# A hybrid attention, MLP and Mamba kernel on one core: smaller first scan parts, and the product with C issued one unit later

## The chip, the core and the metric

The kernel runs on one core of one Trainium2 chip. The core has TensorE (PE, matmuls; PEld are its weight loads), VectorE (DVE), ScalarE (ACT), GpSimd (POOL) and SyncE (SP, here a queue that issues DMAs). Each engine works through its own queue in order and waits on semaphores for the others. The metric is the device time of one execution in microseconds (us), smaller is better. A profile of one execution gives every instruction's start and end.

## The reference, cut to what matters

The input x is 4 batches of 1024 tokens of 128 channels, all float32. Four residual layers follow one another:

```python
x = x + attention(layernorm(x))   # 16 heads, window of 32 tokens and every 64th token before
x = x + mlp(layernorm(x))         # [x, -x] @ +-1 (256x512), relu * 2, @ +-1 (512x512), relu * 2, @ +-1 (512x128)
x = x + mamba(layernorm(x))
x = x + mlp(layernorm(x))

def mamba(x):                     # E = 256 inner channels, N = 16 states, kernel of 4 taps
    xn = layernorm(x) * ln_g + ln_b
    u, z = split(xn @ W_in)
    u2 = silu(causal_conv(u) + conv_b)
    dt_lo, Bm, Cm = split(u2 @ W_xp)              # 8, 16 and 16 columns
    dt = softplus(dt_lo @ W_dt + b_dt)
    for t in tokens:                              # h: (batch, E, N), zero at token 0
        h = exp(dt[t] * A) * h + (dt[t] * u2[t]) * Bm[t]
        y[t] = (h * Cm[t]).sum(over N)
    return res_scale * ((y + u2 * D_param) * silu(z)) @ W_out
```

## The kernel before, in words

**Stages.** Attention runs first, in tiles of 64 rows of two batches at once. Then come the MLP, the Mamba layer and the second MLP, interleaved. Nearly all instructions go through a helper at line 57 (InOrder), so the profile gives line 57 for them, and tiles tell them apart.

**Chunks.** x lies in SBUF as two pairs of batches (bp = 0, 1). A pair is cut into four chunks c of 256 tokens of both batches, 512 columns. The first MLP (early), the second MLP of the first pair (late) and the norm ahead of Mamba (mamba_norm) work on chunks. The MLP's tiles are fxn (normalised), ftp (its transpose in PSUM), fxnT (split in a high and a low part), pf/h1, pg/h2 (the two hidden layers) and pfo; the suffix a, b or c tells early, late and late_batch (the second MLP on single batches). Two lanes run the MLPs of alternating chunks; each is a Python generator of Pieces.

**Parts and units.** The recurrence is scanned in eight parts (parts_in_order, line 911): a part is one batch b and one half f of its tokens, 512 tokens, in the order (0,0), (1,0), (0,1), (1,1), (2,0) ... The first two parts so need chunks 0 and 1. A part has 16 units, one for each state n; 128 units in all. The last column of each state is kept in carry for the batch's second half.

**Before a part.** mamba_pre_half prepares it: gate (pz, SiLU), the convolution as four shifted matmuls (pc) and SiLU to u2, px = u2 @ W_xp, a split of B and C into bf16 parts (bc), B and C written to DRAM (bd), dt (pd, softplus) and du = dt * u2. In the very first part the gate comes last.

**A unit** (scans, from line 1246) does the following, h being the two halves of the 256 channels:
- SP loads B of two states from bd to all partitions (bs, load_b, three units ahead); POOL makes db = du * bs (drive, two units ahead).
- ACT makes da = exp(dt * A) into PSUM (decay), two buffers in all; da of the next unit's h waits until the scan of this unit's h has read it.
- DVE scans each h: hs = da * hs + db.
- PE spreads C over all partitions (pcc, one PSUM buffer), and DVE multiplies hc = hs * pcc. For states 3, 8 and 13 (BY_GP) POOL multiplies instead, with C loaded by SP (cs).
- A DMA on POOL's queue adds each second hc to its neighbour (gather), and PE sums hc into pys with an identity matmul (total). After the last state DVE multiplies the gate with pys (gate_by); then comes the output projection (mamba_out, or mamba_out_own for the second pair).

**The order** within an engine's queue is the program's order while keep is set, which holds for the scans. It comes from a small planner: each unit calls pieces() twice, which issues waiting Pieces of the other work (mamba_pre_half, mamba_norm, mamba_out, statistics, the lanes, in that order), as far as planned times, a rate for each engine (RATES: PE 2.9 us a unit, DVE 1.2, ACT 2.4, POOL 1.2) and three spare PSUM banks allow. Evictions marked lump wait for a call that takes lumps. When a part isn't prepared in time, ready() issues Pieces without regard to rates until it is.

Ahead of the scans all eight PSUM banks are free, and a plain loop runs the norm of chunks 0 and 1, the first preparation and the lanes in turn:

```python
while (*parts_in_order[0], NH - 1) not in prepared:
    ...
    wanted = first[-1].may() and "pe" in first[-1].next.us
    for w in first + ([] if wanted else lanes):
        if w.may():
            w.run()
```

Of the kernel before, what the change touches and what calls it, by code (L numbers as in the profile page):

```python
# [26 lines left out]
P = 128  # L27
# [16 lines left out]
def hybrid_kernel(ctx: ExitStack, tc: tile.TileContext, x, Wq, Wk, Wv, Wo, ln_g, ln_b, W_in, conv_w,  # L44
# [789 lines left out]

    def early(bp, c, *args):
        stats = yield from awaited(("a", bp, c))
        tiles = xs[bp][:, 4 * c : 4 * c + 4, :]
        yield from mlp(f"a{bp}_{c}", tiles, True, *args, hasty=bp == 1 and c < HALF, stats=stats)
        fed.add(("a", bp, c))
# [64 lines left out]
    carry = [mw.tile([P, NH, N], F32, name=f"carry{b2}") for b2 in range(2)]  # L904
# [6 lines left out]
    parts_in_order = [(b, f) for bp in range(NP) for f in range(2) for b in (2 * bp, 2 * bp + 1)]  # L911
# [6 lines left out]
    def mamba_norm(bp, c):  # L918
# [5 lines left out]
        before = order_of[2 * bp, f] - 4  # L924
# [4 lines left out]
        yield Piece(gp=2.7)  # L929

        rs = small.tile([P, 5, 4], F32, tag="rs2", name=f"rs_z{u}", bufs=2)
        gp.tensor_scalar_add(rs[:, 0], mv[:, :, 1], EPS)
        gp.tensor_scalar(rs[:, 1], mv[:, :, 1], 1.0 + EPS, EPS * EPS, ALU.mult, ALU.add)
        both = rs[:, 0:2].rearrange("p a n -> p (a n)")
        gp.tensor_tensor(both, both, minus_half, ALU.pow)
        gp.tensor_scalar_mul(rs[:, 4], mv[:, :, 0], -1.0)
        gp.tensor_mul(rs[:, 2:4], rs[:, 0:2], rs[:, 4:5].to_broadcast([P, 2, 4]))
        gp.tensor_scalar_add(rs[:, 0], rs[:, 0], 1.0)
# [15 lines left out]
        yield Piece(sc=1.6, same=True)  # L954
        ln_apply(tiles, tiles, rs[:, 0], rs[:, 2])
        yield evict(sc=0.6)
# [4 lines left out]
        )  # L961
        fed.add(("n", bp, c))

    def gate_of(v, gate, xnT):
        yield fill(1.8, 2, loose=True)
        pz = [bank(f"pz{v}_{h}") for h in range(NH)]
        for h in range(NH):
            te.matmul(pz[h], w_in[:, E + h * P : E + (h + 1) * P], xnT[:, DC - 1 :], start=True, stop=True)
# [4 lines left out]
    def mamba_pre_half(b, f):  # L973

        bp, b2, place = b // 2, b % 2, order_of[b, f]
        yield Piece(
            ready=lambda: all(("n", bp, c) in fed for c in range(f * HALF, (f + 1) * HALF))
# [4 lines left out]
        xnT = mamba_in[bp, f][:, b2, :]  # L982
        gate = m2.tile([P, NH, CH], F32, name=f"gate{v}", tag="gate", bufs=4)
        if place:
            yield from gate_of(v, gate, xnT)
# [12 lines left out]
        for h in range(NH):  # L998
            for k in range(DC):
# [3 lines left out]
                elif k % 2 == 0:  # L1003
                    yield Piece(pe=1.8, urgent=hurry)
                te.matmul(
                    pc[h], w_conv[:, k, h * P : (h + 1) * P], xnT[:, k : k + CH], start=k == 0, stop=k == DC - 1
                )
        yield evict(lump=True, sc=3.9)
# [18 lines left out]
        if not place:  # L1027
            yield Piece(1, evict=True, ve=1.4)
            ve.tensor_copy(bc, px[: 6 * N])
            ve.tensor_sub(res[: 4 * N], px[: 4 * N], bc[: 4 * N])  # L1030
            yield Piece(-1, urgent=hurry, sc=1.8)
        else:
            yield Piece(1, evict=True, sc=1.8)
            sc.copy(bc, px[: 6 * N])
        sc.copy(dtl[6 * N :], px[6 * N : 6 * N + DR])
        sc.copy(w, px[: 2 * N])
        nc.sync.dma_start(bd, w)
        prepared.add((b, f, "b"))
        if not place:
            sc.copy(bc[: 4 * N], res[: 4 * N])  # L1040
        else:
# [11 lines left out]
        yield evict(lump=True, sc=3.9)  # L1053
        for h in range(NH):
            sc.activation(dt[:, h], pd[h], AF.Softplus, bias=bdt_t[:, h : h + 1])
        if not place:
            ve.tensor_sub(res[: 2 * N], res[: 2 * N], bc[: 2 * N])
        yield urgent(sc=0 if place else 0.6)
        if not place:
            sc.copy(bc[: 2 * N], res[: 2 * N])  # L1060
        for h in range(NH):
            yield urgent(gp=1.3)
            gp.tensor_mul(du[:, h], dt[:, h], u2[:, h])
            prepared.add((b, f, h))
        if not place:
            yield from gate_of(v, gate, xnT)

    def mamba_out(bp, f):

        pair = [(2 * bp + b2, f) for b2 in range(2)]  # L1070
        yield Piece(ready=lambda: all(("g", *k) in fed for k in pair), same=True)
        for q in range(HALF):
            yield fill(2.0)
            po = bank(f"pmo{bp}_{f}{q}")
            for b2 in range(2):
                if b2:
                    yield more(2.0)
                gate = mamba_pre[pair[b2]][0]
                for i in range(4):
                    t0 = (4 * q + i) * R  # L1080
# [399 lines left out]
```

## Time and profile before

| | us |
|---|---|
| median of 3 runs | 893.15 |
| lowest, highest | 889.9, 897.59 |
| the profiled execution | 896.53 |
| its span, first to last instruction | 894.7 |
| last attention instructions, about | 246 |
| first scan starts | 322.9 |
| last scan ends | 852.0 |

Over the whole span PE is busy 757.9 us (85%), DVE 726.9 (81%), POOL 682.5 (76%) and ACT 606.3 (68%). These shares are means over stages with different limits, so the stages are read apart. In a line of groups the columns are engine, operation, tiles out<-in, shapes, count, busy time, mean duration in ns, and the idle time before them with what ended it. In a line of the timeline the first two numbers are the start and the length in us, and the bracket is the idle time of the engine before it. A matmul's end is modelled in the profile, so PE's busy time is not its peak rate. A float32 matmul is two instructions.

### The profile page before, as it was taken

What the parts mean: (1) busy time and instruction counts of PE and PEld (TensorE: products, weight loads), DVE (VectorE), ACT (ScalarE), POOL (GpSimd) and SP (SyncE); (2) the same over time, 40 slices, a digit from 0 to 9 for tenths busy, and PEclk for the clock granted to TensorE, in tenths of its full rate; (3) what the DMA queues carried; (4) which work ended last, traced back from release to release, by engine and by line L of the source; (5) the groups of instructions that cost most, each with busy time, mean ns of one, the idle gap of its engine ahead of it and who ended that gap; (6) DMA issues with size and microseconds to landing.
All of it is one profiled execution on the core that took longest, in us unless ns stands there. A gap on an engine that the chain in (4) does not pass through costs nothing. (4 is left out here: it accounts for less than half of the span.)

```text
span 894.7 us, 16435 instructions
## 1 busy us (share of the span) xinstructions
PE 757.9 (85%) x6204; PEld 465.8 (52%) x6204; DVE 726.9 (81%) x970; ACT 606.3 (68%) x1358; POOL 682.5 (76%) x525
## 2 busy tenths in 40 slices
PE   5798878966788977788989788989889689889898
PEld 2455546645667653334546554535545345656567
DVE  6699998999563258898899998898988779999942
ACT  3776656754364488887878778878967766664523
POOL 6689966999342079999989998979979879877800
PEclk9899989997679989797999999899989799999999
DMA  4743133330010036564564656555565545666410
GB/s 127 129 74 73 27 57 68 74 70 2 3 48 1 1 109 155 127 159 129 137 148 130 153 130 153 145 121 138 155 154 133 141 112 150 164 145 153 108 25 19
DMA packets 59808, 92.77 MB, mean 104 GB/s; under 512 B 6200, under 2 KB 39776, under 8 KB 59728
## 3 DMA queue, kind: packets, MB, share of 16 engines
q1 hardware_dynamic: 49488, 58.15, 22.6%
q0 software_dynamic: 9680, 33.30, 19.8%
q8 instruction: 49, 0.80, 0.4%
q10 hardware_dynamic: 560, 0.26, 0.1%
q14 instruction: 31, 0.25, 0.1%
HBM read 52.11 MB, written 4.72 MB: 64 GB/s over the span
## 5 line engine op out<-in xcount | busy, mean ns | idle before, releaser
L57 POOL TENSOR_TENSOR db<-du,bs 128x1024 f32<-128x1024 f32 x128 | 315.6, 2504 | 23.8 <-DVE hs L57 20.1
L57 ACT ACTIVATE da<-dt,a_t 128x512 f32<-128x512 f32 x256 | 175.2, 687 | 107.1 <-DVE hs L57 106.8
L57 DVE TENSOR_TENSOR_SCAN hs<-da,db 128x512 f32<-128x512 f32 x128 | 149.9, 1209 | 29.7 <-ACT da L57 29.5
L57 DVE TENSOR_TENSOR_SCAN hs<-da,carry,db 128x512 f32<-128x512 f32 x128 | 156.7, 1266 | 5.5 <-ACT da L57 5.2
L57 PE MATMUL pys<-hc,ident 128*128 128x512 f32 x258 | 145.3, 649 | 1.9 <-DMA hc<-hc 1.8
L57 DVE TENSOR_TENSOR hc<-hs,pcc 128x1024 f32<-128x1024 f32 x104 | 126.7, 1218 | 22.1 <-PE pcc L57 15.9
L57 POOL TENSOR_TENSOR prodv<-vS,E 128x128 f32<-128x128 f32 (+14 forms) x30 | 69.6, 2319 | 12.2 <-ACT E L57 11.9
L57 PE MATMUL pga<-h1a,w 128*128 128x512 f32 x256 | 72.4, 435 | 5.1 <-ACT u L57 2.9
L57 PEld LDWEIGHTS pys<-hc,ident 128*128 128x128 f32 x258 | 49.6, 208 | 43.6 <-issue 37.2
L57 POOL TENSOR_TENSOR prod<-kv,qs 128x128 f32<-128x128 f32 (+14 forms) x30 | 71.3, 2376 | 1.0 <-DVE or L57 1.0
L57 POOL TENSOR_TENSOR hc<-hs,cs 128x1024 f32<-128x1024 f32 x24 | 58.1, 2421 | 13.6 <-DVE hs L57 11.6
L57 PE MATMUL pc<-mxnT,w_conv 128*128 128x512 f32 x128 | 63.3, 624 | 4.3 <-DVE h1b L57 2.4
L57 PEld LDWEIGHTS pga<-h1a,w 128*128 128x128 f32 x256 | 51.2, 201 | 27.4 <-issue 4.3
L57 POOL DMA_DIRECT2D hc<-hc x63 | 62.7, 995 | 1.8 <-issue 0.9
L57 ACT ACT_TABLE_LOAD x48 | 61.6, 1283 | 3.5 <-issue 2.6
L57 PE MATMUL pcc<-bc,spread 96*128 96x512 bf16 x104 | 42.0, 404 | 22.5 <-DVE hc L57 21.7
L57 ACT ACTIVATE E<-S 128x512 f32<-128x512 f32 (+15 forms) x62 | 26.5, 472 | 38.8 <-DVE S L57 38.6
L57 PE MATMUL ps<-kx,qT 64*32 64x256 f32 x1008 | 46.2, 432 | 6.3 <-DVE S L57 5.0
L57 POOL TENSOR_TENSOR du<-dt,u 128x512 f32<-128x512 f32 x16 | 24.8, 1551 | 29.7 <-ACT dt L57 29.6
L57 PEld LDWEIGHTS pc<-mxnT,w_conv 128*128 128x128 f32 x128 | 25.2, 199 | 37.4 <-issue 31.9
L57 ACT COPY ep<-pt 128x512 f32<-128x512 f32 x32 | 18.8, 587 | 36.4 <-DVE eo L57 36.1
L57 PE MATMUL pgb<-h1b,w 128*128 128x512 f32 x128 | 38.0, 447 | 1.4 <-ACT u L57 1.4
(245 smaller groups left out, 1682.9 us busy)
## 6 DMA issues: line engine op xcount, KB each, us to landing
bs<-bd SPq DMA_DIRECT2D x64, 512.0 KB
hc<-hc POOLq DMA_DIRECT2D x63, 512.0 KB, 4.6
vr<-vd SPq DMA_DIRECT2D x32, 256.0 KB
cs<-bd SPq DMA_DIRECT2D x24, 256.0 KB
vd<-kv SPq DMA_DIRECT2D x8, 256.0 KB
x<-in_L_attn_a_x_dram SPq DMA_DIRECT2D x15, 128.0 KB
kx<-kT SPq DMA_DIRECT2D x104, 16.0 KB
out_dram<-x SPq DMA_DIRECT2D x8, 128.0 KB
```

The source lines that it names most:

```text
L57: ins = getattr(self.engine, name)(*args, **kwargs)
```

## The change

The first two parts are now called quarters: part (QUARTER, f) holds tokens f*256 to f*256+255 of batches 0 and 1 side by side, 512 columns as before. Quarter 0 needs chunk 0 alone, quarter 1 chunk 1. Chunk 0's MLP is cut in two: each lane takes two of its four tiles (256 columns). The lanes then take chunks (0,1), (0,3), (1,1), (1,3) and (0,2), (1,0), (1,2). A scan of a quarter is two instructions of 256 columns, one for each batch. mamba_norm marks a chunk as transposed ("t") ahead of its residual copy, and Mamba's preparation waits for that mark. For the first chunk some small norm operations go from POOL to DVE. In the first part the order within the preparation is another: dt's projection comes before the copy of B and C to DRAM, the small casts of bc go to POOL, du goes to DVE, and db of unit 0 is made half by DVE and half by POOL. The loop before the scans is replaced by one that runs both lanes until chunk 0 is through, and then puts norm and preparation first.

In the scans, DVE's product of unit i-1 now stands between unit i's two scans; before, the product of unit i stood behind both. The two calls of pieces() move with it: the one that takes lumps comes behind the product, the other at the unit's end; pcc is issued between them. The planner's durations of scans and products are a little smaller.

```diff
+    def early_half(lane, *args):
+        stats = yield from awaited(("a", 0, 0))
+        at = slice(2 * lane, 2 * lane + 2)
+        yield from mlp(f"a0_0{lane}", xs[0][:, at, :], True, *args, stats=stats[:, :, at])
+        fed.add(("half", lane))
+        if all(("half", k) in fed for k in range(2)):
+            fed.add(("a", 0, 0))
...
-        yield from mlp(f"a{bp}_{c}", tiles, True, *args, hasty=bp == 1 and c < HALF, stats=stats)
+        yield from mlp(f"a{bp}_{c}", tiles, True, *args, hasty=c == 1 or (bp == 1 and c < HALF), stats=stats)
...
-    parts_in_order = [(b, f) for bp in range(NP) for f in range(2) for b in (2 * bp, 2 * bp + 1)]
+    QUARTER = "quarter"
+    QT = CH // 2
+    parts_in_order = [(QUARTER, 0), (QUARTER, 1)]
+    parts_in_order += [(b, f) for bp in range(NP) for f in range(2) for b in (2 * bp, 2 * bp + 1)][2:]
...
-        yield Piece(gp=2.7)
+        by = ve if bp + c == 0 else gp
+        yield Piece(gp=2.9 if by is ve else 2.7)
...
+        needs = [("t", 0, f)] if b == QUARTER else [("t", b // 2, c) for c in range(f * HALF, (f + 1) * HALF)]
...
         for h in range(NH):
             te.matmul(pd[h], w_dt[6 * N :, h * P : (h + 1) * P], dtl[6 * N :], start=True, stop=True)
-        yield evict(lump=True, sc=3.9)
+        if not place:
+            yield Piece()
+            sc.copy(w, px[: 2 * N])
+            nc.sync.dma_start(bd, w)
+            prepared.add((b, f, "b"))
+            ve.tensor_copy(bc, px[: 6 * N])
+            ve.tensor_sub(res[: 4 * N], px[: 4 * N], bc[: 4 * N])
+            gp.tensor_copy(bc[: 4 * N], res[: 4 * N])
+            ve.tensor_sub(res[: 2 * N], res[: 2 * N], bc[: 2 * N])
+            gp.tensor_copy(bc[: 2 * N], res[: 2 * N])
+        yield evict(lump=True, sc=3.9 if place else 1.9)
...
         for h in range(NH):
-            yield urgent(gp=1.3)
-            gp.tensor_mul(du[:, h], dt[:, h], u2[:, h])
+            yield urgent(gp=1.3) if place else urgent(ve=0.6)
+            (gp if place else ve).tensor_mul(du[:, h], dt[:, h], u2[:, h])
...
+        def product(i):
+
+            if i < 0 or by_gp(i):
+                return
+            hss[i] = m2.tile([P, NH, CH], F32, name=f"hc{i}", tag="hc", bufs=6)
+            ve.tensor_tensor(
+                hss[i], hs_of.pop(i), pcs.pop(i).unsqueeze(1).to_broadcast([P, NH, CH]), ALU.mult
+            )
+            done["hc", i] = done["pcc read",] = spend("ve", 1.15, *after(("pcc", i)))
+
...
+            def scan(h):
+                da = das.pop((i, h))
+                spans = [(b2, slice(b2 * QT, (b2 + 1) * QT)) for b2 in range(2)] if b == QUARTER else [(b, slice(0, CH))]
+                for b2, ts in spans:
+                    first = carry[:, h, b2 % 2, n : n + 1] if f else 0.0
+                    ve.tensor_tensor_scan(hs[:, h, ts], da[:, ts], db[:, h, ts], first, ALU.mult, ALU.add)
+                us = (1.21 if f else 1.15) + 0.07 * (len(spans) - 1)
+                done["hs", i, h] = spend("ve", us, *after(("da", i, h), ("db", i)))
+                decay(i + 1, h)
+
+            scan(0)
+            done["da", i + 1, 0] = spend("sc", 0.67, *after(("hs", i, 0)))
+            product(i - 1)
             if gather(i):
                 spend("gp", 0.9, *after(("hc", i - 1)))
+            t = times["ve"]
+            pieces(t + 1.5)
             if not by_gp(i):
-                pc = wide.tile([P, CH], F32, name=f"pcc{i}", tag="pcc")
-                te.matmul(pc, spread[: 6 * N, n, :], mamba_pre[b, f][4], start=True, stop=True)
+                pcs[i] = wide.tile([P, CH], F32, name=f"pcc{i}", tag="pcc")
+                te.matmul(pcs[i], spread[: 6 * N, n, :], mamba_pre[b, f][4], start=True, stop=True)
                 done["pcc", i] = spend("pe", 0.4, *after(("pcc read",)))
-            hs = m2.tile([P, NH, CH], F32, name=f"hs{i}", tag="hs")
-            db = dbs.pop(i)
-            for h in range(NH):
-                first = carry[b % 2][:, h, n : n + 1] if f else 0.0
-                ve.tensor_tensor_scan(hs[:, h], das.pop((i, h)), db[:, h], first, ALU.mult, ALU.add)
-                done["hs", i, h] = spend("ve", 1.235 if f else 1.175, *after(("da", i, h), ("db", i)))
-            decay(i + 1, 0)
-            done["da", i + 1, 0] = spend("sc", 0.67, *after(("hs", i, 0)))
-
-            t = times["ve"]
-            pieces(t + 2.5, lumps=False)
...
+            scan(1)
...
-                ve.tensor_tensor(hss[i], hs, pc.unsqueeze(1).to_broadcast([P, NH, CH]), ALU.mult)
-                done["hc", i] = done["pcc read",] = spend("ve", 1.205, *after(("pcc", i)))
...
             done["sum", i] = spend("pe", total(i))
             t = times["ve"]
-            pieces(t + 2.2)
+            pieces(t + 2.0, lumps=False)
+        product(last)
...
-            early(0, lane, f1, lane, *[in_scan_buffers] * lane),
-            early(0, 2 + lane, f1, lane),
-            early(1, lane, f1, lane),
-            early(1, 2 + lane, f1, lane),
+            early_half(lane, f1, lane, *[in_scan_buffers] * lane),
+            *(early(bp, c, f1, lane) for bp, c in (((0, 1), (0, 3), (1, 1), (1, 3)), ((0, 2), (1, 0), (1, 2)))[lane]),
...
-        while (*parts_in_order[0], NH - 1) not in prepared:
+        while ("a", 0, 0) not in fed:
...
+        while (*parts_in_order[0], NH - 1) not in prepared:
+            w = lead if ("t", 0, 0) not in fed else pre
+            if not w.count:
+                w.since = lead.since
+            issue(w)
+            if pre.held and lead.next:
+                issue(lead)
+            if aside and (QUARTER, 0, "b") in prepared:
+                aside = False
+                for v in lanes:
+                    while v.next.evict or v.held:
+                        issue(v)
+            for v in lanes:
+                while aside and v.may() and max(ends(v)[0].values(), default=0.0) < w.since + 0.3:
+                    issue(v)
```

## The prediction

> **What bounds the kernel now.** I read the page first, for the span and the slices (each digit is a fortieth, 22.4 us).
>
> ```profile
> span 894.7 us, 16435 instructions
> DVE  6699998999563258898899998898988779999942
> POOL 6689966999342079999989998979979879877800
> ```
>
> VectorE (DVE) is full except in slices 11 to 15: the stretch from the end of attention (246 us) to the first scan. The table by stages shows what fills that stretch and what fills the scans.
>
> ```profile
> 323.00:388.00 65.00, 51.06 (x128) 23.46 (x128) 55.42 (x62) 57.34 (x120) 60.80 (x49) 0.82 0.48 127
> 388.00:457.00 69.00, 58.24 (x173) 29.64 (x172) 60.46 (x60) 56.19 (x127) 62.19 (x44) 0.90 0.59 149
> 457.00:588.00 131.00, 116.44 (x444) 68.61 (x443) 120.66 (x113) 107.48 (x231) 120.47 (x96) 0.94 0.56 141
> 588.00:723.00 135.00, 117.98 (x418) 63.61 (x418) 112.94 (x108) 105.06 (x242) 118.12 (x89) 0.92 0.56 141
> 723.00:852.00 129.00, 114.73 (x480) 71.65 (x479) 124.61 (x126) 79.31 (x144) 104.71 (x64) 0.95 0.57 139
> 262.00:323.00 61.00, 57.65 (x273) 42.98 (x272) 12.97 (x33) 31.19 (x57) 10.80 (x16) 0.97 0.07 23
> ```
>
> Columns after the length: PE, PEld, DVE, ACT, POOL busy with instruction counts, PE's granted clock, DMA share, GB/s. Before the scans PE is the bound (57.65 of 61) and DVE waits. From 322.9 to 852.0, 529 us for 128 units of 4.13 us, DVE is busy 474 (90%), POOL 466, PE 458, ACT 405. The scans are a DVE stage with 55 us of holes; the groups say which.
>
> ```profile
> L57 DVE TENSOR_TENSOR_SCAN hs<-da,db 128x512 f32<-128x512 f32 x128 | 149.9, 1209 | 29.7 <-ACT da L57 29.5
> L57 DVE TENSOR_TENSOR hc<-hs,pcc 128x1024 f32<-128x1024 f32 x104 | 126.7, 1218 | 22.1 <-PE pcc L57 15.9
> ```
>
> So the holes are a late decay from ACT or a late spread C from PE, never POOL. After 852 comes a fixed tail of 42.7 us (last gate, output projection, last MLP).
>
> **Step 1, the head.** Now the first part needs batch 0's tokens 0 to 511, that is chunks 0 and 1: two whole MLPs and two norms. After the change it needs chunk 0 alone, each lane taking half. What two halved lanes cost stands in the tail, where the last chunk is run just so (256 columns):
>
> ```profile
> 258.63 15.09 PE L57 MATMUL pga<-h1a,w 128*128 128x512 f32 x64
> 273.56 7.30 PE L57 MATMUL pfoa<-w,h2a 128*128 128x128 f32 x64
> ...
> 877.87 2.13 PE L57 MATMUL pfc<-fxnTc,w 128*128 128x256 f32 x16 [0.33 <-ACT fxnTc L57]
> 879.84 7.73 PE L57 MATMUL pgc<-h1c,w 128*128 128x256 f32 x64
> 887.41 3.73 PE L57 MATMUL pfoc<-w,h2c 128*128 128x128 f32 x32
> 891.18 0.48 DVE L57 SCALAR_TENSOR_TENSOR ox<-pfoc,total,ox 128x256 f32<-128x256 f32 x1 [1.30 <-PE pfoc L57]
> ```
>
> The first two lines are the pair of whole chunks, the rest the halved pair: 891.66 - 877.87 = 13.8 us from first projection to residual. Now the first MLP gets its split input at 254.3 (DVE is making spread and w_conv until 253.6; that stays), and its residuals end at 281.65. New: 254.3 + 13.8 = 268.1.
>
> Norm of chunk 0: 8 statistics 1.75, small ops with the power on POOL 2.9, apply 1.65, last transpose 0.2, scaled copy 0.77, waits 0.3: 7.6, so 275.7. (Putting the 4-element ops on DVE saves at most the 1.2 of POOL's four; I take nothing.) Now the convolution starts only at 300.98.
>
> Convolution to first scan, now 21.95 us (300.98 to 322.93): conv 7.0, SiLU 0.7, px 1.9, then dt rows and w copied (0.6 each), bd to DRAM until SP issues bs (313.38 to 315.02, 1.64), bs landing, half of db 1.2. Landing of bs isn't shown: at most 5.2 (issued 315.02, db at 320.21 waited for du, not for it), at least 2.1 (the small loads on POOL's queue); I take 4.6, what the equally large hc gathers need. Sum 18.2: first scan at 294. The other branch (pd 2.0, softplus 1.3, du on DVE 1.3, db 0.7 after px) is shorter, and the two bc casts that go to POOL (no row of such a cast; between the 0.36 of POOL's small copy into mxnT and the 1.55 of du) end before bs is there. Without that cover they cost up to 3 us. bd and bs keep their order on SP; bd now stands behind the pd matmuls, 0.6 later than dt's rows. **First scan 29 us earlier**, bounds 20 (PE's fill between norm and convolution, 4 us now, grows; bs 5.2) to 34.
>
> **Step 2, the product one unit late.** In the timeline of DVE:
>
> ```profile
> 544.25 1.22 DVE L57 TENSOR_TENSOR hc<-hs,pcc 128x1024 f32<-128x1024 f32 x1
> 545.38 2.45 DVE L57 TENSOR_TENSOR_SCAN hs<-da,carry,db 128x512 f32<-128x512 f32 x2
> 547.93 1.22 DVE L57 TENSOR_TENSOR hc<-hs,pcc 128x1024 f32<-128x1024 f32 x1
> 549.07 2.45 DVE L57 TENSOR_TENSOR_SCAN hs<-da,carry,db 128x512 f32<-128x512 f32 x2
> ```
>
> The scan begins 0.08 us before the product in front of it has ended (544.25 + 1.22 = 545.47), the two scans overlap as much, but the product begins 0.09-0.10 after the scan that it reads. That read of a result just written costs 0.09 + 0.08 = 0.173. In the whole trace 73 of 104 products follow a scan directly; the others already have another instruction between. The late product reads scans of a unit ago: 73 x 0.173 = **-12.6 us**, bounds 0 (something else holds the unit) and 104 x 0.173 = -18.
>
> The Trainium skill, page VectorE: DVE Perf Modes, section The DRAIN you can't avoid, speaks against this: chained copies with and without a semaphore between took the same time, so the dependence would cost nothing. By it this step is 0 and the sum below 12.6 worse; the rows differ, and I go by them.
>
> Behind the product on DVE's queue now stands the unit's second scan, so a late pcc holds that scan instead of the next unit's first; pcc still has two scans (2.5 us) between its buffer's release and its use, so the 15.9 us stay. The gather on POOL needs product i-1, now done 2.4 us into unit i; POOL reaches it after db (2.38). Its wait is 0 to 0.5, at most 31 us over 63 gathers, hidden in POOL's 63 us of idle time; if POOL had none, it would cost just that.
>
> **Step 3, shorter scans.** In the first 32 units each scan of 512 becomes two of 256: 64 more. No scan of 256 is in the trace. Others on DVE: h1c takes 0.417 at 256 columns and 0.673 at 512, fxnTc 0.40 and 0.67, so two halves cost 0.13 to 0.16 more, less the 0.08 overlap; the operand carry adds 0.05 (1.266 - 1.209) in half of them. 64 x 0.08 + 32 x 0.05 = **+6.6**, bounds 1.3 (0.02 each) and 10 (0.16).
>
> **Step 4, work pushed into the scans.** Before 322.9 DVE now does the evictions of chunks 0 and 1 and most of 2 and 3. After, at the scan start chunk 0 is done and chunks 1 and 2 are past their first projections. A chunk is 0.67 + 4 x 0.68 + 0.75 = 4.1 us of DVE, its norm 1.75: chunk 1 leaves 1.4 + 1.75, chunk 2 1.4, chunk 3 3.4: **+8**, bounds 4 and 12. On PE some 30 us move. I cost them at nothing, because lanes now have a hole: chunk 3's output is at 335.7, and the next fxna is at 384.7; PE is busy only 51 of the 65 us. Without the hole they'd cost what rival D says.
>
> **Step 5, the second part is late.** It now waits for chunk 1's MLP, norm and preparation. At the scan start chunk 1 lacks 4 x 2.05 + 2 x 2.0 = 12.2 us of planned PE, chunk 2 as much, and a unit is allowed 2.9: both end near unit 8 or 9. Norm takes two units (7.6), so preparation starts near unit 11 to 13, and load_b asks for it at 13. From there the rest is issued at once. Its chain was 22 us in the head, against three units (12 us) already queued: DVE stands **+10**, bounds 0 and 26 (preparation in the scans took 335.7 to 374.3, 38.6). Chunk 3 has until unit 29; no standstill taken there.
>
> **Sum.** -29 - 12.6 + 6.6 + 8 + 10 = -17. The profiled execution took 896.53 (span 894.7 and 1.8 around it): 879.5. The median is 893.15, 3.4 lower: **876 us**. Runs of before spread from 889.9 to 897.6, so a difference within 1% (9 us) can hardly be told from none.
>
> **The rivals.** B, clean hand-over: chunk 1 runs faster than planned, since the planner's PE figures are a little generous (2.05 for 8 pga matmuls that take 15.09/64 each, 1.89), step 5 is 0, and with pieces at two points a unit 7 of the 55 us of holes go: 893 - 34 = 859. For it: ACT and PE aren't full in 323:388. Against: clock 0.82 there.
>
> C, the start is given back: the chain of step 5 takes its 38.6 us, so +26 instead of +10: 892. For it: pieces wait for three spare PSUM banks, and two lanes and the preparation want two each. Against: once forced, nothing else is issued.
>
> D, slower, PE becomes the bound: PE is busy 109 of the 134 us of 323:457. With 30 more it needs 139; the granted clock there is already 0.82 and 0.90, and at a tenth less it needs 139 / 0.9 = 154, 20 over; lanes then reach the end a halved chunk later (13.8 more in the tail). 876 + 20 + 13.8 = 910. It decides once more than 25 us of PE move. Against: a convolution matmul shows 0.59 of busy time while they start 0.43 apart, so busy PE is less than full. That the change doesn't do what it says isn't likely: the first scan's place is set by what it waits for.
>
> **From cases to numbers.** A (forecast, 876) 0.48, B 0.18, C 0.17, D 0.17. B and nearly all of A are faster by over 1% (0.64), C and some of A within (0.19), D slower (0.17). All steps at their good ends give 893 - 47 = 846, all at their bad ends 893 + 28 = 921; they have separate causes, so A's own range takes half of each side, 861 to 898. The range takes in A's range, B's value and C's, short of D's: 857 to 899.
>
> **What would show it.** First hs near 294; median product starting 0.08 before its predecessor's end; 320 scans, those of 256 near 0.66 to 0.72; a DVE hole of some 10 us between 345 and 365 waiting for ACT da; the tail still 42 to 43 us. The prediction is wrong if the first scan is later than 303, if part two stands over 26 us, or if the last scan to the end is over 50.

## The result, and the profile after

The changed kernel takes 942.77 us (median of four runs, 939.52 to 945.51) against 891.74 of the kernel before beside it: a ratio of 1.0559, interval 1.0498 to 1.062. It is slower by 51 us; the prediction was 876, range 857 to 899. Two of the kernels below, plan_only and head_lanes, were profiled in an execution at a far lower granted clock (0.809 and 0.187) than their others, so only their times are used.

The page after, its span and two rows of the slices (a slice is now 23.5 us):

```profile
span 941.2 us, 16652 instructions
DVE  6799999998527961998188998599988799999222
POOL 6799948996406973798187899599998799885000
```

The dip ahead of the scans is shorter, as meant. Three things are new: a 1 in slice 16 and another in slice 20, inside the scans, and three 2s at the end in place of one 4 and one 2. The table by stages gives them lengths (columns as in the prediction: PE, PEld, DVE, ACT, POOL busy, PE's granted clock, DMA share, GB/s).

```profile
293.00:382.00 89.00, 62.62 (x187) 32.81 (x186) 56.38 (x91) 62.78 (x156) 66.44 (x60) 0.81 0.36 94
382.00:475.00 93.00, 78.92 (x274) 45.38 (x273) 67.27 (x108) 57.65 (x120) 62.00 (x49) 0.88 0.40 100
...
867.00:941.00 74.00, 62.63 (x417) 53.77 (x415) 18.71 (x50) 21.72 (x55) 2.98 (x6) 0.90 0.05 15
```

The first two rows are the two parts of 256 tokens. Before, the first two parts took 65.5 and 68.5 us; now 89.1 and 93.2. No engine is full in them, so something waits. The last row is the tail: 74 us in which PE works 63 and VectorE 19. From the trace, the times of three marks:

| | before | after | difference |
|---|---|---|---|
| first scan starts | 322.9 | 292.6 | -30.3 |
| first to last scan | 529.1 | 574.2 | +45.0 |
| last scan to the end | 42.6 | 74.4 | +31.8 |
| span | 894.7 | 941.2 | +46.5 |

("First to last scan" is called the stage below, "last scan to the end" the tail.) Not all of the first row is the change's: attention, which it doesn't touch, ends earlier in this trace, and the first MLP's norm starts on ACT at 242.7 instead of 246.3. From there to the first scan it is 76.6 us before and 49.9 after, 26.7 less. Traces of six kernels below whose head is the old one (late_only, late_room, late_lanes, before_lanes, late_hs3, plan_tight) have their first scan between 318.8 and 322.7.

In the middle row VectorE's busy time hardly changes (474.2 to 476.1); its idle time goes from 54.9 to 98.0. The timeline shows where it stands, VectorE from the end of unit 13 on and again from unit 30 on (start, length, engine, line, operation; in brackets the idle time ahead and what ended it):

```profile
344.21 1.26 DVE L57 TENSOR_TENSOR_SCAN hs<-da,db 128x256 f32<-128x256 f32 x2
370.65 2.43 DVE L57 TENSOR_TENSOR_SCAN hs<-da,db 128x256 f32<-128x256 f32 x4 [25.18 <-issue]
378.24 1.27 DVE L57 TENSOR_TENSOR_SCAN hs<-da,db 128x256 f32<-128x256 f32 x2 [5.16 <-ACT da L57]
...
463.59 2.67 DVE L57 TENSOR_TENSOR_SCAN hs<-da,carry,db 128x256 f32<-128x256 f32 x4 [20.52 <-issue]
471.18 1.39 DVE L57 TENSOR_TENSOR_SCAN hs<-da,carry,db 128x256 f32<-128x256 f32 x2 [4.92 <-ACT da L57]
```

VectorE stands still for 25.2 and 5.2 us in units 14 and 15, while the second part is prepared, and in the same way for 20.5 and 4.9 in units 30 and 31, ahead of the third: 55.8 us together. "issue" names no releaser, so the engine that the scan waits for has to be followed. The decay ended on ACT just before 370.65. ACT in the same stretch:

```profile
345.04 0.30 ACT L57 ACTIVATE waste<-x 128x128 f32<-128x128 f32 x1
...
353.66 0.19 ACT L57 ACTIVATION_READ_ACCUMULATOR waste<-x,st_fa 128x1 f32 x1
353.75 1.06 ACT L57 ACTIVATE h2a<-pga 128x512 f32<-128x512 f32 x2
...
369.87 0.69 ACT L57 ACTIVATE da<-dtquarter,a_t 128x512 f32<-128x512 f32 x1
```

and PE:

```profile
344.25 1.02 PE L57 MATMUL pzquarter<-mxnT,w_in 128*128 128x512 f32 x2
354.38 2.08 PE L57 MATMUL pzquarter<-mxnT,w_in 128*128 128x512 f32 x2 [9.11 <-ACT h2a L57]
```

Between 345.0 and 353.7 ACT computes statistics (stats_ahead) of chunks of the second pair, which nobody needs yet. ready() had been called in unit 13 and issued whatever was able. Behind them stands the eviction h2a; the trace names it as what released the second half of the second part's gate matmuls (pz, 354.4) after 9.1 us of idle PE. From the source, h2a empties a PSUM bank, and the preparation may only go on when one is spare. Then the preparation runs undisturbed, pz to the decay at 369.9, 15.5 us. The third part has no such block behind its norm, and is still late: chunk 3's residual lands at 427.9, its transposed norm at 446.3, and the db that the third part starts with begins 24 us after that.

The tail, on PE:

```profile
883.50 5.87 PE L57 MATMUL pgc<-h1c,w 128*128 128x512 f32 x24
889.21 4.02 PE L57 MATMUL pfoc<-w,h2c 128*128 128x128 f32 x32
...
907.74 6.03 PE L57 MATMUL pgc<-h1c,w 128*128 128x256 f32 x32
```

pgc and pfoc are late_batch, the lanes' second MLP of the last two batches. Before, the chunks of 512 columns among them had ended by 852, and only halved ones stood in the tail. How late the lanes run can be read from one tile: the residual x of the last chunk of the first MLP ends at 581.0 before and at 671.6 after. (This is the lanes' mark below, "last early x" in the tables.)

The groups of the two operations that the prediction counted on:

```profile
L57 DVE TENSOR_TENSOR hc<-hs,pcc 128x1024 f32<-128x1024 f32 x104 | 124.3, 1195 | 4.0 <-PE pcc L57 3.8
L57 DVE TENSOR_TENSOR_SCAN hs<-da,db 128x256 f32<-128x256 f32 (+1 forms) x128 | 114.9, 938 | 46.4 <-issue 25.2
```

The product's idle time fell from 22.1 to 4.0 us: locally the late product does what it should.

### The profile page after: what moved, and what is told of

Read it like the earlier page. It is cut to its first block, busy times and chain, and to the rows that moved or that the text cites. A ratio compares the mean times of both kernels' runs of the same rounds, so it can differ in the third digit from the quotient of the medians.

```text
span 941.2 us, 16652 instructions
## 1 busy us (share of the span) xinstructions
PE 761.4 (81%) x6244; PEld 466.8 (50%) x6244; DVE 730.2 (78%) x1048; ACT 606.0 (64%) x1361; POOL 682.3 (72%) x520
## 5 line engine op out<-in xcount | busy, mean ns | idle before, releaser
L57 POOL TENSOR_TENSOR db<-du,bs 128x1024 f32<-128x1024 f32 x96 | 239.2, 2526 | 16.8 <-DVE hs L57 11.4
L57 DVE TENSOR_TENSOR_SCAN hs<-da,carry,db 128x512 f32<-128x512 f32 (+1 forms) x192 | 201.8, 1088 | 39.4 <-issue 20.5
L57 ACT ACTIVATE da<-dt,a_t 128x512 f32<-128x512 f32 x192 | 131.4, 687 | 86.3 <-DVE hs L57 85.6
L57 DVE TENSOR_TENSOR_SCAN hs<-da,db 128x256 f32<-128x256 f32 (+1 forms) x128 | 114.9, 938 | 46.4 <-issue 25.2
L57 PE MATMUL pys<-hc,ident 128*128 128x512 f32 x194 | 104.1, 623 | 1.8 <-DMA hc<-hc 1.8
L57 POOL TENSOR_TENSOR db<-duquarter,bs 128x1024 f32<-128x1024 f32 (+1 forms) x32 | 78.2, 2472 | 6.9 <-DVE hs L57 4.9
L57 PE MATMUL pga<-h1a,w 128*128 128x512 f32 (+1 forms) x288 | 76.7, 418 | 5.7 <-DVE h1a L57 5.5
L57 POOL TENSOR_TENSOR prodv<-vS,E 128x128 f32<-128x128 f32 (+14 forms) x30 | 69.6, 2321 | 11.7 <-ACT E L57 11.5
L57 ACT ACTIVATE da<-dtquarter,a_t 128x512 f32<-128x512 f32 x64 | 43.8, 687 | 37.3 <-DVE hs L57 37.2
L57 PEld LDWEIGHTS pys<-hc,ident 128*128 128x128 f32 x194 | 37.3, 198 | 51.3 <-issue 39.7
L57 PE MATMUL pc<-mxnT,w_conv 128*128 128x512 f32 x96 | 44.8, 601 | 0.0
L57 ACT COPY ep<-pt 128x512 f32<-128x512 f32 x32 | 18.8, 587 | 35.5 <-DVE eo L57 35.2
```

The source lines that it names most:

```text
L57: ins = getattr(self.engine, name)(*args, **kwargs)
```

## The experiments

Three questions: which half of the change costs, what makes the tail longer, and where VectorE's saving goes. Theory at the start: the change's two halves don't affect each other, the late product gains some 10 us and the halved parts lose the rest to the standstills. All ratios are to the kernel before in runs beside it, with the 95% interval.

### One half at a time

**late_only** has the late product and no halved parts; the planner's numbers are those of the change.

```
-   te.matmul(pc ...); scan 0; scan 1; pieces(t + 2.5, lumps=False); product(i); pieces(t + 2.2)
+   scan 0; product(i - 1); pieces(t + 1.5); te.matmul(pc ...); scan 1; pieces(t + 2.0, lumps=False)
+   planned scan 1.21 / 1.15, product 1.15   (before: 1.235 / 1.175, 1.205)
```

> The unit's new order alone, on the parts and the head of the kernel before; the two calls of the planner have the changed kernel's allowances (1.5 and 2.0). Theory: the 0.173 us of each of the 73 products that follow their scan directly is DVE time on the bound, so the span falls by 9 to 13 us, to 878 to 884 beside 891.7 of before; first scan at 323, tail 43. Rival 1 (something else holds the unit): within 4 us of before. Rival 2 (the new order or its smaller allowances are what starves the lanes in the changed kernel): the last chunk of the first MLP ends far later than 580, the tail grows by 20 us or more, and the time is over 900.

Measured 925.64 us, ratio 1.037 (1.0355 to 1.0386). First to last scan 526.1 (before 529.1), VectorE's busy time in it down 13 us to 460.9 (in part because the lanes' evictions moved out of it), and the tail 77.8 in place of 42.6. So the half that should have gained loses 33 us, all in the tail, and rival 2 held.

**late_room** is late_only with the old allowances (`t + 2.5`, `t + 2.2`), **quarters_only** is the changed kernel with the unit's old order and numbers, **after_room** the changed kernel with the old allowances.

> As late_only, with the allowances of before (2.5 and 2.2) at the two calls of the planner. Theory: the lanes aren't held by the allowance, so within 5 us of late_only. Rival 2: 10 us or more faster than late_only, with an earlier end of the lanes' work.

> The quarters and the new head with the unit order of before. Theory: standstills of DVE ahead of the second and third part of 45 to 60 us together and a tail of 65 to 80 us come from the parts, so they are all here; the product's wait on its scan is back, so 950 to 956. Rival 2: standstills or tail shrink by 20 us or more and the time is under 930.

> The changed kernel with the allowances of before (2.5 and 2.2) at the two calls of the planner. Theory (lanes are late because two parts now need chunks that no earlier stage has made, and because a standstill issues nothing of theirs): within 8 us of 942.8, tail still over 65. Rival 2 (allowance): tail at most 55, time 915 to 930.

| | time, us | ratio | first scan | scans | tail | last early x |
|---|---|---|---|---|---|---|
| late_only | 925.64 | 1.0370 (1.0355-1.0386) | 320.4 | 526.1 | 77.8 | 645.1 |
| late_room | 913.75 | 1.0242 (1.0218-1.0265) | 321.2 | 537.3 | 51.9 | 620.1 |
| quarters_only | 932.19 | 1.0451 (1.0422-1.0480) | 295.1 | 573.2 | 65.2 | 658.4 |
| after_room | 951.07 | 1.0658 (1.0641-1.0676) | 293.7 | 585.4 | 70.8 | 663.8 |

Either half alone is slower, and each makes the tail longer: by 35.2 us (late_only) and 22.6 (quarters_only), against 31.8 with both, so the two do not add. The halved parts bring standstills without the late product too (12.4 and 20.5 us, the largest of quarters_only), but quarters_only is 10.6 us faster than the full change, not 7 to 13 slower as expected: there too the late product, with its plan, costs. A little more allowance helps late_only by 12 us, as rival 2 said, and the full change not at all (951.07, just outside its theory's 8 us).

### The tail: the lanes' plan

**late_lanes** is late_only with much more room for the lanes; **before_lanes** gives the same room to the kernel before, as a control; **plan_only** and **plan_tight** take the other way, the kernel before with the change's numbers.

```
late_lanes, before_lanes:  RATES pe 2.9 -> 4.0; pieces(t + 4.5) in both places
plan_only:                 planned scan 1.21 / 1.15, product 1.15
plan_tight:                plan_only, and pieces(t + 1.5), pieces(t + 2.0)
```

> late_only with more room for the lanes: PE's rate 4.0 instead of 2.9 a unit and allowances of 4.5 at both calls of the planner. Instructions are the same, the MLP's stand earlier among the scans. Theory (the product's wait was DVE time, but the shorter planned unit pushed MLP work out of the scans into the tail): the tail falls from 78 to 43 to 50 us, the scan stage is 525 to 545, the time 887 to 903 beside 925.6 of late_only. Rival (the order itself is slow: hs has two buffers and scans now wait for POOL's product): over 910, with the loss inside the scan stage.

> The kernel before with the same room for the lanes (rate 4.0, allowances 4.5). Control: if the lanes of before were not held back, within 8 us of before (884 to 900). If more room is a gain of its own, under 884; then late_lanes has to be compared with this kernel.

> The kernel before with nothing but the planner's durations of the changed one (scans 1.21 and 1.15, product 1.15); the order of scans and product is untouched. Theory (planned DVE time is the budget for MLP work in a unit): the lanes are later, the tail grows by 5 to 20 us, the time is 896 to 912. Rival (the planned durations don't matter): within 4 us of before.

> The kernel before in its own unit order, with only the numbers of the plan that the change brought: planned scan and product 1.21, 1.15 and 1.15 us (as in plan_only) and the allowances 1.5 and 2.0 us in place of 2.5 and 2.2. Theory, that the smaller allowance of the first call holds the lanes' matmuls back: the stage of the scans shortens to 520-526, the tail grows from 42.6 to 50-75, time 900-915. Rival, that the allowance only decides beside the new order of the calls: tail 40-47, time 882-893, as in plan_only.

| | time, us | ratio | scans | tail | last early x |
|---|---|---|---|---|---|
| late_lanes | 893.32 | 1.0027 (1.0006-1.0048) | 526.8 | 42.7 | 578.4 |
| before_lanes | 891.95 | 1.0015 (0.9994-1.0037) | 529.6 | 36.3 | 585.3 |
| plan_only | 885.05 | 0.9939 (0.9915-0.9962) | | | |
| plan_tight | 894.02 | 1.0021 (0.9994-1.0047) | 526.8 | 45.5 | 601.2 |

late_lanes settles the tail of late_only: three numbers of the plan, no instruction of the work, bring it from 77.8 back to 42.7, and the lanes' mark back to 578. The expectation for plan_only (896 to 912) was a miss, and plan_tight's rival held but for 1 us: in the old order the change's numbers cost nothing in time, though the lanes' mark comes 20 us later (601.2). So neither the planned durations nor both changes of numbers together make the old order slower; with the new places of the two calls the same numbers cost 33 us. Which step of the planner joins the two, and which of the three numbers undoes it, was not separated.

**after_mend** applies this to the full change: the room of late_lanes, the norm's Pieces of the first pair marked urgent, and no stats_ahead in a forced call during the first two parts.

```
+ RATES pe 4.0, pieces(t + 4.5) twice
+ yield Piece(..., urgent=not bp)              # three Pieces of mamba_norm
+ if forced and w is works[4] and now[0] < 2 * PER: continue
```

> The changed kernel with the lanes' room of late_lanes, the norms of the first pair's chunks let past the rates, and no statistics of the second pair issued while a part is waited for in the first two parts. Theory: tail 45 to 55 instead of 74; the standstills ahead of the second and third part shrink only a little, since the chain from transposed chunk to du is as long: 40 to 56 us; time 905 to 925. Rival (the standstills come from what is issued in front of the chain): under 20 us of standstill and under 900.

Measured 904.44 us, ratio 1.0162 (1.012 to 1.0205): 38 us of the 51 are back, past the good end of its theory in time, tail and standstills, and short of the rival's. The tail is 44.4, the standstills 11.7 + 4.7 + 13.4 + 4.9 = 34.7 in place of 55.8. Against late_lanes the head gains 26.6 (294.4 against 321.0), the stage of the scans loses 39.7 (566.5 against 526.8). The standstills are 34.7 of that. The three edits went in together, so what each is worth was not measured.

**mend_gate** moves pz and its two SiLU evictions of the second and third part behind the part's preparation (`if place: gate_of` becomes `if place > 2`, the call at the end takes the rest).

> after_mend, with the gate's two matmuls (2.1 us of PE) and their two Silu evictions (on ACT) of the second and third part moved behind the part's preparation, as the first part has it. Theory, that the standstills are in-order queues ahead of the preparation's steps: the four standstills sum to 24-31 us in place of 34.7, first to last scan 556-564, time 893-902. Rival, that the chunk's x comes too late and the chain behind it waits for other things than the gate: sum within 3 us of 34.7, time 901-908.

The standstills fell to 10.0 + 5.2 + 9.7 + 4.4 = 29.2 (from the unrounded values), as the theory said, and the time rose to 924.66, ratio 1.0363 (1.0317 to 1.0408): the tail is 57.4 and the lanes' mark 641.8 (after_mend 615.4). A miss on the time: the stage stayed at 568.5, and the lanes were later again. Why moving two matmuls and their evictions does that was not followed.

### Where VectorE's saving went

late_lanes is the late product without the long tail, and its stage is 526.8 against 529.1. Even these 2.3 us are not clear: plan_tight, in the old order, has the same 526.8. VectorE's idle time by gap, from before to late_lanes, says where the saving goes. Gaps under 0.2 us (a product behind its scan) fell from 7.3 to 1.7, busy time from 474.2 to 470.0; gaps over 0.2 us grew from 47.7 to 55.1. Its waits in the chain of waits (engine, tile, releaser: us, times, longest):

```profile
DVE hc L57 <- PE pcc L57: 20.8, 23, 2.5
...
DVE hs L57 <- ACT da L57: 16.8, 17, 2.2
...
DVE hs L57 <- POOL hc L57: 13.7, 9, 3.4
```

In before, pcc's wait was 15.9 us, and da's 34.7, of which 8.3 stand ahead of the first scan and not in the stage. The third line is new: hs has two buffers, GpSimd's product (states 3, 8 and 13) holds one, and with no product of its own behind the second scan VectorE comes sooner to the scan that overwrites it. **late_hs3** takes that wait away: `tag="hs", bufs=3`, and hc five buffers in place of six for the room.

> The late product with the lanes' allowance of late_lanes, and three buffers for hs in place of two (hc five in place of six, to make room). Theory, that the gain of the late product was lost to the scan's wait for GpSimd's product of every fifth unit, which holds one of only two hs buffers: that wait (13.7 us in late_lanes) falls under 2 us, the stage of the scans from 527 to 513-521 us, the time to 880-888. Rival, that ACT's decays and PE's spread set the pace anyway and the wait only changes its name: waits for da and pcc grow by as much, the stage stays at 524-530, the time at 889-898.

Measured 888.29, ratio 0.997 (0.9946 to 0.9995). The wait is gone, and the stage is 526.1, as the rival said; the time lies between the two bands.

```profile
DVE hc L57 <- PE pcc L57: 29.6, 32, 2.4
...
DVE hs L57 <- ACT da L57: 19.0, 20, 2.1
```

pcc and da took 11 of the 13.7 us over (29.6 - 20.8 and 19.0 - 16.8). **before_half** and **late_half** ask whether VectorE sets the stage at all.

```
- ve.tensor_tensor(hss[i], hs, pc ...)
+ ve.tensor_tensor(hss[i][:, :, : CH // 2], hs[:, :, : CH // 2], pc[:, : CH // 2] ...)
```

> The kernel before, in which VectorE's product with C computes the first 256 of 512 tokens only (PE's sum reads these twice, and the gather moves half): 104 products of about 0.67 us in place of 1.2, 55 us less on VectorE, every instruction in the same order and with the same plan. Theory A, VectorE bounds the stage: 529 falls to 474-490, time 838-855. Theory B, the stage is bound by several engines in turn (GpSimd 466 us busy, PE 459, ACT 405, in-order queues between them): the stage falls by less than half of that, to 503-520, time 865-885, and VectorE's waits for da and pcc grow.

> late_hs3 with the same halved product: 55 us less on VectorE in the order in which the product stands one unit late. Theory A: stage 526 to 471-487, time 835-852. Theory B: stage 500-518, time 862-882. If before_half gains and late_half does not, the late order has another bound than the order before.

before_half: 870.68, ratio 0.9753 (0.9703 to 0.9803), stage 507.6. late_half: 874.69, 0.9803 (0.9756 to 0.9851), stage 510.5. VectorE is busy 53 and 52 us less in the stage, and 21.5 and 15.6 us arrive (late_half against late_hs3). The page's groups of before_half:

```profile
L57 POOL TENSOR_TENSOR db<-du,bs 128x1024 f32<-128x1024 f32 x128 | 342.9, 2822 | 4.7 <-DVE hs L57 4.4
...
L57 POOL DMA_DIRECT2D hc<-hc x63 | 99.8, 1585 | 0.7 <-issue 0.4 <-POOL hc L57 0.3
```

GpSimd is busy 487.2 of the 507.6 us, 96%, with 4.7 us of idle time ahead of db (before: 23.8). Theory B's figures held in both, with one reserve: the records of the halved gather sum to 37 us more than those of the whole one (62.7 before), and db went from 2504 ns to 2822. The two lie partly over each other, and GpSimd's busy time rose by 21 us (466.4 to 487.2), so the experiment loaded GpSimd as it relieved VectorE, and the stage could not have come near theory A's 474. What it shows is that a VectorE with 53 us less to do runs into the others: in before_half its waits for da and pcc grew by 7.2 and 4.4 us, and 13.2 us of waiting for GpSimd's product, which holds an hs buffer, appear in the old order too. Where the stage would end without the load on GpSimd stays open; the test without such a load is late_hs3.

### Keeping the head's gain without halved parts

The change also shortened the first part's preparation (dt ahead of the copies of B and C, du and half of the first db on VectorE, the norm's small operations on VectorE). **head_short** is plan_only with these edits alone.

> No halved parts, no late product: plan_only with the changed kernel's edits to the first part's preparation alone (dt before the copies of B and C, du and half of the first db on VectorE, the gates of the first two chunks' norm on VectorE, the transposes evicted before the residual's norm). Theory, that the head's gain has a share that costs no standstill because the whole first half of the tokens is still normalized before the first scan: first scan from 322.9 to 308-315, stage 527-532, tail 40-46, time 872-882. Rival, that the first chunks' x is what the head waits for, or that the lanes' matmuls that ran beside the head are now left for later: first scan at 316-322 or the tail longer by the gain, time 883-892.

Measured 901.19, ratio 1.011 (1.008 to 1.014), first scan 323.2: nothing gained, 1.7% above plan_only by the ratios, and both theories' bands missed. Where the loss of time lies wasn't followed; ACT shows why the first scan didn't move:

```profile
314.94 0.60 ACT L57 ACTIVATE h2a<-pga 128x512 f32<-128x512 f32 x1 [0.95 <-PE pga L57]
...
320.54 0.60 ACT L57 ACTIVATE h2a<-pga 128x512 f32<-128x512 f32 x1 [1.26 <-PE pga L57]
321.15 1.28 ACT L57 ACT_TABLE_LOAD   x1
322.45 1.30 ACT L57 ACTIVATE da<-dt,a_t 128x512 f32<-128x512 f32 x2
```

dt is ready at 314.0, but four evictions of the lanes, each waiting for PE, stand ahead of the first decay in ACT's order. **head_aside** empties the lanes once the two chunks are normalized, and holds them until the part is prepared.

```
+ if all(("t", 0, c) in fed for c in first_half):
+     for w in lanes: run while w.next.evict or w.held
+     wanted = True
```

> head_short, with the two lanes emptied when the two normalized chunks stand ready, and held until the first part is prepared, so that no Gelu eviction stands on ACT ahead of the first decays (in head_short four of them, the last ending at 321.1, a table load, and the decay at 322.4). Theory: the first scan goes from 323 to 312-317 and the lanes' matmuls of these 20 us (about 10 us) end in the tail, which goes from 45 to 45-56: time 888-900. Rival, that emptying the lanes holds the convolution by as much: first scan 319-324, time 898-908.

```profile
304.39 1.26 ACT L57 ACTIVATE dt<-pd,bdt 128x512 f32<-128x512 f32 x2
305.67 1.28 ACT L57 ACT_TABLE_LOAD   x1
306.96 1.30 ACT L57 ACTIVATE da<-dt,a_t 128x512 f32<-128x512 f32 x2
```

(The evictions h2a apply Relu; "Gelu" in the expectation is a slip.) The first scan comes at 309.5, 13.4 us earlier and with no standstill later; attention ends 3.6 us earlier in this trace, so some 10 of the 13.4 are the edits'. The stage is 520.6, and the tail 57.8. 890.85, ratio 0.9976 (0.9953 to 1.0). The time is in the theory's band; the first scan came earlier than its band and the tail is 1.8 us over. What ends the gain is shown: the scans end 22 us earlier, and the tail grows by 15, with 32 of pgc's 512-column matmul instructions now behind the last scan, where before had none. That these are the matmuls which the head gave up isn't shown: the lanes' mark came earlier (563.1) than before (581.0).

**head_lanes** gives head_aside the room of late_lanes; **head_late** adds the late product with three buffers for hs. **head_lanes_again** is head_lanes run once more, for its stages.

> head_aside with the lanes' allowances at 4.5 us and PE's rate at 4.0, as in before_lanes. Theory, that the lanes' delay is the plan's and the stage has room for it: first scan 308-312, stage 524-531, tail 38-47, time 872-885. Rival, that PE's matmuls of the first 20 us have no room in the stage: what the tail gets back the stage grows by, time within 5 us of head_aside (886-896).

> head_lanes with the product one unit late and three buffers for hs (late_hs3's order). Theory, that the order of the product is worth nothing to the stage whose length GpSimd, PE and ACT set along with VectorE: within 4 us of head_lanes. Rival, that the 13 us that it frees on VectorE come through when the lanes have room: 5-13 us less than head_lanes.

> head_lanes once more, for a profile that can be read. If the late product makes the difference to head_late (876 us, first scan 312.6, stage 519.9, tail 42.0): first scan 308-313, tail 40-48, and the stage 540 or more, with waits for da and pcc that the late order doesn't have. If the lanes do: stage 518-526 and tail 58-70. If the head does: first scan 320 or later. Time 895-905 again in each case.

| | time, us | ratio | first scan | scans | tail |
|---|---|---|---|---|---|
| head_aside | 890.85 | 0.9976 (0.9953-1.0000) | 309.5 | 520.6 | 57.8 |
| head_lanes | 901.16 | 1.0088 (1.0055-1.0121) | | | |
| head_lanes_again | 902.31 | 1.0106 (1.0072-1.0140) | 312.6 | 544.2 | 43.5 |
| head_late | 876.01 | 0.9802 (0.9782-0.9823) | 312.6 | 519.9 | 42.0 |

head_lanes missed its theory's time (872 to 885), and head_lanes_again came out as its first case said. Both theories of head_late missed: the late product, with its third hs buffer and its places of the planner's calls, is worth 25 us here, 24 of them in the stage. The waits for the spread C, first of head_lanes_again:

```profile
DVE hc L57 <- PE pcc L57: 38.9, 32, 2.9
```

and of head_late:

```profile
DVE hc L57 <- PE pcc L57: 23.4, 26, 3.3
```

15.5 of the 24 us are this wait: with more of the lanes' matmuls among the scans the spread C comes late, and less late in the new order. Why it does stays open: in both orders two scans lie between the release of pcc's one buffer and its use, and without the head's edits the same room parted the two orders by only 2.8 us of stage (before_lanes 529.6, late_lanes 526.8). The moved calls, which decide what PE does ahead of pcc, were not tried by themselves. Shown is the combination: with the late product the room takes 16 us off the tail (57.8 to 42.0) at no cost to the stage, without it 14 at a cost of 24. head_late beats both kernels: 1.98% below the kernel before.

## Why the prediction was wrong, by its steps

**Step 1, the head: right, the last digits by luck.** The first scan was predicted at 294 and came at 292.6, but attention ended 3.6 us earlier in this trace than in the one that the sum started from. The head itself became 26.7 us shorter in place of 29, inside the bounds. The halved residuals ended at 263.8 and 265.6 in place of 268.1; from the convolution to the first scan it took 20.1 in place of 18.2.

**Step 2, the product one unit late: the local price right, the conclusion wrong.** 99 of 104 products now start before their predecessor's end, by 81 ns in the median, as worked out, where a dependent one started 0.09 after. The Trainium skill, in VectorE: DVE Perf Modes, The DRAIN you can't avoid, found that a semaphore between chained copies costs nothing extra; for this pair, a product that reads the scan ahead of it, the rows show 0.17 us, and the measurement decides. But the sum took 12.6 us off the end. late_lanes gave at most 2.3 at the stage (526.8 against 529.1): 9.8 freed, 4.2 of busy time and 5.6 of small gaps, against 7.4 more of waits. The list of holes was misread in size, too: of the 29.5 us for da, 8.3 stand ahead of the first scan, outside the stage. "Never POOL" held only as long as VectorE came late enough; the two buffers of hs were not listed among what the new order touches. And the new places of the planner's calls, with its new numbers, cost late_only 33 us in the tail, which no step had.

**Step 3, shorter scans: right.** Two scans of 512 without carry take 2.33 us in a row; four of 256 take 2.42 in the first quarter and 2.66 in the second, which now reads a carry. Over 16 units each that is 1.4 and 5.3, 6.7 us together in place of 6.6. The two parts of the term each missed a little: a split costs 0.045 without and 0.105 with carry in place of 0.08, the carry 0.06 in place of 0.05.

**Step 4, work pushed into the scans: wrong at "I cost them at nothing".** VectorE's share was small (+1.9 us of busy time in the stage, with step 2's saving in it). For PE's share the sum had nothing, on the ground of the lanes' hole after 336; but the lanes' mark slid by 91 us, and the "fixed tail" grew by 31.8. quarters_only, without the late product, has 22.6 of tail from the halved parts and the work they move; late_only has 35.2 from the other half alone. How the 31.8 divide is open. The text had named the price if that cover went, rival D, but with PE full as its condition. PE was busy 474.6 of the 574 us. For the late product late_lanes shows that the plan held the lanes while PE had time; for the full change after_mend points to it (tail 44.4), but there the plan's room came with two other edits.

**Step 5, the second part late: the time of the call right, the wait and its size wrong.** load_b asked at unit 13, as said. But not "three units already queued": only the scans of unit 13 itself followed, since the decays of unit 14 and later stand behind the forced Pieces on ACT. And "from there the rest is issued at once" left out what is issued with it: 9 us of statistics ahead of the eviction that the preparation needed. +10 was 30.3. "No standstill taken" at the third part was 25.4 more; its chunk got its residual at 427.9, 91 us later than before (336.4). Rival C had this place and 26 us for one part.

Sum, by the marks of the two traces: -30.3 at the head, 55.8 of standstills, 31.8 of tail, and -10.8 for all the rest of the stage make 46.5. Its three conditions for being wrong were well chosen; two came true (a part standing over 26 us, a tail over 50).

## What to carry to other kernels

A busy share of 90% on one engine doesn't make its savings arrive: look how busy the next one is (here 88%, 87% and 77%) and which buffers it holds, and expect the waits to change names. Work taken out of a stage that bounds on PE has to be given a place: read the free time of the place it moves to, and read what lets it be issued there, for an order written ahead holds back work though the engine is free. And when a first stage is cut in two to start sooner, the second half's whole chain must fit behind the first half's work, with the in-order queues of every engine on it; here 35 us of standstill were left in after_mend and 29 in mend_gate, and the 27 us at the head were spent.

## What was not expected

The order in which the lanes' matmuls are issued moved the time by more than half of VectorE's products: late_only and late_lanes execute the same work, with three numbers of the plan different, and lie 32 us apart, while 53 us less on VectorE brought before_half 22. And a gather of half the data, two runs of 256 columns in each partition in place of one of 1024, took 1585 ns to issue on GpSimd in place of 995, with db beside it 13% longer (2822 against 2504); the runs don't show why.
